# A chain of WKV layers and a graph convolution on one core: r ahead of the sums, inverses and norms ahead of what can wait

## The chip, the cores and the metric

The kernel runs on one core of a Trainium2 chip. The metric is the device time of one execution in microseconds (us); the times shown are medians of several runs. One more execution was taken with the hardware profiler, and all engine times below are from that one. PE is the matrix engine, DVE the vector engine, ACT the scalar engine, POOL is GpSimd, SP issues most DMAs. Each engine works its instructions off in the order of the program and waits for the others by semaphores.

## What is computed

The input x has 16 images of 192 channels and 56 x 56 positions, in float32. Three layers of one kind follow each other, then a graph convolution. Cut to what matters:

```python
xn = group_norm(x, 32)                      # before every layer
k, v, r = xs @ Wk.T, xs @ Wv.T, xs @ Wr.T   # xs: tokens (3136) by channels of xn
x_bi = 0.5 * (wkv(w, u, k, v) + flip(wkv(w, u, flip(k), flip(v))))
h = layernorm(sigmoid(r) * x_bi)
x = x + h @ Wo.T                            # three times, then:
xj = max over rolls by +-2 rows and columns of xn, minus xn, at least 0
x = x + gelu(batchnorm(concat(xn, xj) @ conv_w.T))
```

`wkv` is a running weighted mean over the tokens: numerator p and denominator q are sums of exp(k) v and exp(k) that decay by a constant per channel at every token, and the token itself counts with a bonus.

## The kernel before, in words

Two images make a pair: channels 0 to 127 of each and the two remaining blocks of 64 fill three rows of 128 partitions. The 3136 tokens are cut into seven chunks of 448. A *run* is one layer of one pair. It has a forward pass, chunks 0 to 6 (`A`), that makes exp(k), exp(k) v, the forward scans and their quotient, and a backward pass, chunks 6 to 0 (`B`), that makes r, the backward scans, their quotient, the gate, the layer norm, the output product and the residual. The convolution has one pass of seven chunks (`C`). Eight pairs go in two streams, so that the backward pass of one stream's run stands beside the forward pass or the convolution of the other's.

A written-out list of steps sets the whole order; no scheduler moves anything. Each step calls one of these functions (line numbers of the profile), and the order of the calls in it is the order on every engine:

- `both_a` (L1323), a backward chunk beside a forward chunk: 85 steps, chunks 4 to 0 of a backward pass. `both_a_first` (L1379) is the same for the first pair of chunks of a layer, chunk 5: 17 steps.
- `both_c` (L1426), a backward chunk beside a chunk of the convolution: 42 steps, six a layer, chunks 5 to 0.
- `forward_a`, `forward_c`, `backward_alone`: chunks that have no partner. `conv_part` (L1503) puts halves of delayed convolution products into forward steps.

The pieces that the change moves:

- `b_gate` (L986): PE's product r of a backward chunk, seven matmuls; `b_exp` (L989): ACT's exponentials of it (L996); `b_sigmoid` (L1001): the rest of the sigmoid on ACT (L1003, L978).
- `b_q`, `b_p`, `a_q`, `a_p`: three scans each on DVE (L875). `b_den`, `b_num`, `a_den`, `a_num`: the bonus on DVE (L890). `a_keys`, `a_values`: PE's products k and v; `a_exp` (L920), `a_ekv` (L940) read them.
- `ln` (L974) and `exp_minus` (L977): the inverse as exp(-log) on ACT (L975, L978).
- `b_mix` (L1028): nine products and sums on POOL (L1031 to L1033). `a_y` (L980): one on POOL (L982).
- `b_squares` (L1037): ACT squares (L1040). `b_sums` (L1042): eight matmuls into one bank `st` (L1047, L1049). `b_rs1`: the square of the means on ACT (L1055); `b_rs2`: one matmul that takes it from the mean squares (L1059); `b_rs3`: logarithm and exponential on ACT (L1063, L1065); `b_spread`: three matmuls that spread the result over the partitions (L1071, tile `rsb`); `b_scale`: DVE multiplies (L1076); `b_out`: the output product `ops` on PE; `b_x` (L1085): DVE adds the residual (L1089), SP stores the chunk (L1094).
- `gap` (L822) does one of four parts of the next run's norm: `norm_sums` (DVE, then PE's small product `psg`), `norm_var` (DVE, ACT), `norm_fold` (small operations, then ACT folds the factor into the weights of k and v, L770), `norm_fold_r` (POOL folds it into those of r, L772).
- `c_product`: half of the convolution's product on PE (tile `cv`), with xn or with the maxima; `c_rows`, `c_columns`: the maxima on DVE (L1114 to L1129); `c_gelu`: ACT (L1150), with a load of another function table before and after; `c_add` (L1157): POOL adds x (L1159); `store` (L1172): four DMAs on SP.
- `count` takes statistics of a later pair's input on ACT (L734, L735), up to two thirds of a chunk in a paired step.

PE's results go to seven PSUM banks, handed out in the order of the program; chunks in SBUF take one of 33 slots.

The core of a paired step before, since the prediction follows its order:

```python
        b_gate(*nback[1:]); b_exp(*nback[1:])     # r of the next chunk back
        count(z); b_q(*b)
        b_rs2(*l); b_rs3(*l)                      # l: the chunk of the step before
        b_sigmoid(*b)
        a_values(*a)
        b_spread(*l)
        ...
        b_squares(*b, (1,))
        b_sums(*b)
        ...
        b_rs1(*b)
        invert(den())
```

## Time and profile before

| | |
|---|---|
| median of 3 runs | 5217.34 us (5207.3 to 5221.48) |
| profiled execution | 5220.16 us, span 5218.2 us |
| mean granted clock of PE | 0.935 |
| ACT, POOL busy | 71%, 55% of the span |
| DMA | 482.47 MB, 92 GB/s, queue of SP 28.5% of 16 engines |

The steps can be found in the trace by their instructions. From the first DVE instruction of a step to that of the next they take:

| kind of step | number | mean us | DVE busy in it |
|---|---|---|---|
| both_a | 85 | 25.3 | 24.4 |
| both_a_first | 17 | 30.4 | 27.3 |
| both_c | 42 | 25.3 | 22.3 |
| forward steps (A and C) | 80 | 13.9 | 12.7 |
| backward_alone | 24 | 11.2 | 10.6 |

How to read it: a timeline line holds the start in us, the duration in us, the engine, the line of the kernel, the operation with output, inputs and shapes, and how many instructions were merged; the bracket at its end is the idle time of that engine just before, and what ended it. PEclk is the share of full speed at which PE was clocked in a stretch; 1.00 is full, 0.50 half.

### The profile page before, as it was taken

Reading aid. Unit: us, or ns where it says so; the run is one execution under the profiler, and the core shown is the slowest. Engines: PE = TensorE matmul, PEld = TensorE weight load, DVE = VectorE, ACT = ScalarE, POOL = GpSimd, SP = SyncE. Lnnn points to the kernel's source line nnn. Section 1 sums busy time; section 2 is a strip of 40 time slices with the busy share of each in tenths; the row PEclk is TensorE's granted clock in tenths of the full one; section 3 lists DMA queues with packets and bytes.
Section 4 is the critical chain, followed back from the end, with each engine's and each line's share of the span. In section 5 each row is a group of like instructions: output and inputs, shape, how many; then the busy total and the mean of one; then the engine's idle time right before and its main releaser. Section 6 shows DMA issues by size and latency. Waiting matters only on the chain. (4 is left out here: it accounts for less than half of the span.)

```text
span 5218.2 us, 51856 instructions
## 1 busy us (share of the span) xinstructions
PE 4733.3 (91%) x15542; PEld 1498.8 (29%) x15542; DVE 4750.5 (91%) x6271; ACT 3684.6 (71%) x7163; POOL 2889.2 (55%) x2251
## 2 busy tenths in 40 slices
PE   7899998989899999998989999999898999999897
PEld 3222222223232222222323222222232322222222
DVE  6999999998989999999898999999889899999995
ACT  6777787776566777787656678777756667777772
POOL 1665665554545656565454556556545455666562
PEclk8999999999899999999989999999998999999998
DMA  5222222233232222223233223222333322222233
GB/s 154 69 82 87 90 86 89 85 110 97 90 116 72 87 90 93 82 90 122 93 93 101 84 75 100 88 85 87 128 93 101 93 74 77 72 84 77 80 104 120
DMA packets 314274, 482.47 MB, mean 92 GB/s; under 512 B 66432, under 2 KB 306688, under 8 KB 313984
## 3 DMA queue, kind: packets, MB, share of 16 engines
q1 hardware_dynamic: 312832, 477.59, 28.5%
q8 instruction: 126, 2.06, 0.2%
q10 hardware_dynamic: 1152, 1.48, 0.1%
q14 instruction: 164, 1.34, 0.1%
HBM read 324.83 MB, written 154.14 MB: 92 GB/s over the span
## 5 line engine op out<-in xcount | busy, mean ns | idle before, releaser
L875 DVE TENSOR_TENSOR_SCAN q<-fdecays,ek 128x449 f32<-128x449 f32 (+1 forms) x1008 | 1023.4, 1068 | 28.0 <-ACT ek L920 25.4
L875 DVE TENSOR_TENSOR_SCAN p<-fdecays,ekv 128x449 f32<-128x449 f32 (+1 forms) x1008 | 1020.3, 1065 | 0.6
L982 POOL TENSOR_TENSOR p<-p,q 128x1344 f32<-128x1344 f32 x168 | 512.0, 3047 | 830.3 <-ACT q L978 546.9
L1031 POOL TENSOR_TENSOR ekv<-ekv,ek 128x448 f32<-128x448 f32 x504 | 602.7, 1196 | 456.1 <-ACT ek L978 385.3
L1033 POOL TENSOR_TENSOR p<-p,sg 128x448 f32<-128x448 f32 x504 | 638.0, 1266 | 57.2 <-ACT ek L884 12.7
L1032 POOL TENSOR_TENSOR p<-p,ekv 128x448 f32<-128x448 f32 x504 | 606.1, 1203 | 39.5
L1040 ACT ACTIVATE ek<-p 128x448 f32<-128x448 f32 x504 | 286.4, 572 | 309.4 <-POOL p L1033 308.9
L886 POOL COPY ekv<-p 128x3 f32<-128x3 f32 x282 | 233.1, 827 | 488.0 <-DVE p L875 457.2
L1076 DVE TENSOR_TENSOR p<-p,rsb 128x448 f32<-128x448 f32 x504 | 282.4, 613 | 194.5 <-PE rsb L1071 194.4
L920 ACT ACTIVATE ek<-k,k 128x448 f32<-128x448 f32 x504 | 297.2, 632 | 225.3 <-PE k L601 179.2
L735 ACT ACTIVATE fjunk<-x 128x448 f32<-128x448 f32 x672 | 387.7, 577 | 40.1 <-DVE x L1089 13.4
L1071 PE MATMUL rsb<-rs,fpicks 32*128 32x448 f32 (+1 forms) x1008 | 359.2, 629 | 42.4 <-ACT rs L1065 42.4
L1159 POOL TENSOR_TENSOR ml<-ml,x 128x1344 f32<-128x1344 f32 x56 | 178.9, 3194 | 391.8 <-ACT ml L1150 391.8
L890 DVE SCALAR_TENSOR_TENSOR ek<-ek,fcc,q 128x896 f32<-128x896 f32 x336 | 379.1, 1167 | 0.0
L890 DVE SCALAR_TENSOR_TENSOR q<-ek,fcc,q 128x896 f32<-128x896 f32 x336 | 359.2, 1109 | 6.3 <-ACT cvb L954 4.6
L1089 DVE SCALAR_TENSOR_TENSOR x<-ops,fwob,x 128x448 f32<-128x448 f32 x504 | 314.2, 670 | 46.7 <-PE ops L601 26.6
L734 ACT ACTIVATE fjunk<-x 128x448 f32<-128x448 f32 x600 | 342.5, 571 | 11.4
L996 ACT ACTIVATE sg<-r,r 128x448 f32<-128x448 f32 x504 | 313.0, 627 | 33.5 <-PE r L607 20.7
L890 DVE SCALAR_TENSOR_TENSOR ekv<-ekv,fcc,p 128x896 f32<-128x896 f32 x336 | 330.1, 1022 | 0.0
L940 DVE SCALAR_TENSOR_TENSOR ekv<-v,v,ek 128x448 f32<-128x448 f32 x504 | 312.5, 672 | 16.6 <-PE v L601 8.0
L975 ACT ACTIVATE q<-q 128x1344 f32<-128x1344 f32 x168 | 221.5, 1318 | 125.5 <-DVE q L890 101.3
L890 DVE SCALAR_TENSOR_TENSOR p<-ekv,fcc,p 128x896 f32<-128x896 f32 x336 | 295.3, 919 | 6.5 <-POOL ekv L886 1.7
(235 smaller groups left out, 11546.4 us busy)
## 6 DMA issues: line engine op xcount, KB each, us to landing
x<-xd SPq DMA_DIRECT2D x240, 672.0 KB, 5.3
xd<-x SPq DMA_DIRECT2D x168, 672.0 KB, 3.9
x<-in_x_dram SPq DMA_DIRECT2D x320, 224.0 KB, 4.3
x<-in_x_dram SPq DMA_DIRECT2D x320, 112.0 KB, 4.2
out_dram<-ml SPq DMA_DIRECT2D x112, 224.0 KB, 2.3
m<-xd SPq DMA_DIRECT2D x112, 168.0 KB, 5.1
wkv<-in_wfold_dram SPq DMA_DIRECT2D x24, 640.0 KB, 5.6
out_dram<-ml SPq DMA_DIRECT2D x112, 112.0 KB, 2.3
```

Source lines behind the costliest of these rows:

```text
L734: S.activation(junk, xt[:, j, :], AF.Identity, accum_out=stats[:, 0, j, c : c + 1])
L735: S.activation(junk, xt[:, j, :], AF.Square, accum_out=stats[:, 1, j, c : c + 1])
L875: V.tensor_tensor_scan(out, dec[:, column(j)].to_broadcast([P, L if first else L + 1]), e, 0.0, ALU.mult, ALU.add)
L890: by_channel(lambda js, i: V.scalar_tensor_tensor(dst.t[:, js, :], e.t[:, js, :], cc[:, i : i + 1], state.t[:, js, :], ALU.mult, ALU.add))
L940: V.scalar_tensor_tensor(e.t[:, j, :], ps[j][:, 0:L], b[:, j, :], run.ek[c].t[:, j, :], ALU.add, ALU.mult)
L982: G.tensor_mul(run.h[c].t, run.h[c].t, den.t)
L996: S.activation(sg.t[:, j, :], ps[j][:, 0:L], AF.Exp, bias=b[:, j, :], scale=-1.0, accum_out=run.chk[:, at : at + 1])
L1031: G.tensor_mul(y.t[:, j, :], y.t[:, j, :], den.t[:, j, :])
L1032: G.tensor_add(h.t[:, j, :], h.t[:, j, :], y.t[:, j, :])
L1033: G.tensor_mul(h.t[:, j, :], h.t[:, j, :], sg.t[:, j, :])
L1071: PE.matmul(ps[j][:, :L], pick[rows, j, :], rs[rows, :], start=True, stop=True)
L1089: V.scalar_tensor_tensor(xj, ps[j][:, 0:L], wob[:, column(j)], xj, ALU.add, ALU.add, accum_out=run.new[:, 0, j, c : c + 1] if c == 0 else ...
```

## The change

In `both_a`: r of the chunk after the next (`far`) is computed just ahead of `b_sums`, where it belongs to the same run; `b_gate` skips a chunk that is done. Since only chunks 4, 3 and 2 have such a `far`, chunk 4's step computes two r and those of chunks 1 and 0 none. `a_values` moves ahead of `b_rs2` and `b_rs3`, `count` behind them. The sigmoid moves between the two parts of the inverse, and the forward inverse goes ahead of `b_rs1`.

In `both_a_first` the forward scan and value product go ahead of the denominators, the forward denominator and its inverse ahead of the scaling, the scaling and output product ahead of the next k.

In `both_c` the three gaps (parts of the norm) stand earlier, `b_rs1` and `b_rs2` stand between the logarithm and the exponential of the inverse, and `c_add` behind `b_mix`. In the last step beside a convolution, where a forward pass follows, both halves of its product go to `conv_part`, as those of chunk 6 did before. `fresh` keeps `gap` from folding weights whose load was only just issued.

In `backward_alone` the fold stands right behind the inverse. `c_add` calls `store` before it adds its own result to the list, so that no older result is left there.

```diff
     def gap(eng=V):
-        if norms:
+        if norms and norms[0][0] is norm_fold and norms[0][1] in waiting + fresh:
+            fresh.clear()
+        elif norms:
             part, run = norms.pop(0)
...
     def b_gate(run, c):
-        product(run, "r", run.w[2], run.xb[c], c == NL - 1)
+        if once(run, "r", c):
+            product(run, "r", run.w[2], run.xb[c], c == NL - 1)
...
             require_all(run.chk, slice(3 * NL + 9, NCHK))
+        store()
         stores.append((run, c, g))
...
-    def both_a(b, a, nback, nfront, z, loads):
+    def both_a(b, a, nback, nfront, z, loads, far):
...
-        count(z)
-        b_q(*b)
+        a_values(*a)
         if l:
             b_rs2(*l)
             b_rs3(*l)
-        b_sigmoid(*b)
-        a_values(*a)
+        count(z)
+        b_q(*b)
         if l:
             b_spread(*l)
         b_p(*b)
         b_den(*b)
-        for js in (AC, slice(1, 2)):
-            ln(b[0].ek[b[1]], js)
-            exp_minus(b[0].ek[b[1]], js)
+        ln(b[0].ek[b[1]], AC)
+        exp_minus(b[0].ek[b[1]], AC)
+        b_sigmoid(*b)
+        ln(b[0].ek[b[1]], slice(1, 2))
+        exp_minus(b[0].ek[b[1]], slice(1, 2))
...
         b_squares(*b, (1,))
+        if far:
+            b_gate(*far[1:])
         b_sums(*b)
         a_p(*a)
         gap()
         a_den(*a)
+        invert(den())
         b_rs1(*b)
         late[b] = 0.5
-        invert(den())
         gap()
...
     (both_a_first)
         b_p(*b)
+        a_q(*a)
+        a_save(*a)
+        a_ekv(*a)
+        b_squares(*l, (1,))
         b_den(*b)
         invert(b[0].ek[b[1]])
...
-        a_ekv(*a)
-        b_squares(*l, (1,))
         if nback is not None:
             b_gate(*nback[1:])
         b_sums(*l)
         b_rs1(*l)
+        b_rs2(*l)
+        b_rs3(*l)
         if nback is not None:
             b_exp(*nback[1:])
-        a_q(*a)
-        b_rs2(*l)
-        b_rs3(*l)
+        a_p(*a)
+        a_den(*a)
+        invert(den())
+        spread_and_scale(l)
         keys(nfront)
-        a_p(*a)
-        spread_and_scale(l)
         b_squares(*b, (0,))
-        a_save(*a)
         exp_keys(nfront)
         b_squares(*b, (2, 1))
         b_sums(*b)
-        a_den(*a)
+        a_num(*a)
         b_rs1(*b)
         late[b] = 0.5
-        invert(den())
-        a_num(*a)
         add(l)
...
     (both_c)
             b_out(*l1)
+        gap()
...
         b_den(*b)
-        invert(b[0].ek[b[1]])
+        ln(b[0].ek[b[1]])
+        gap()
         if l0:
             b_rs1(*l0)
             b_rs2(*l0)
+        exp_minus(b[0].ek[b[1]])
+        if l0:
             b_rs3(*l0)
-        gap()
-        if half:
-            u = half.pop()
-            c_gelu(*u, False)
-            c_add(*u)
+        ended = half.pop() if half else None
+        if ended:
+            c_gelu(*ended, False)
...
-        if not first:
+        ahead = l0 and nback is None and nfront is not None and nfront[0] == "A"
+        if not first and not ahead:
             c_product(*a, 0)
         c_rows(*a)
-        gap()
         c_columns(*a)
         gap()
         b_num(*b)
         b_sigmoid(*b)
         b_mix(*b)
+        if ended:
+            c_add(*ended)
...
+        elif ahead:
+            a_q(*nfront[1:])
+            a_save(*nfront[1:])
+            a_values(*nfront[1:])
+            b_scale(*l0)
+            b_out(*l0)
+            late[l0] = 2
+            convs.extend(((a, 0), (a, 1)))
         else:
...
     (backward_alone)
         invert(b[0].ek[b[1]])
+        gap(G)
         b_sigmoid(*b)
         b_p(*b)
-        gap(G)
         b_num(*b)
...
+            far = steps[i + 2][0] if nback is not None and i + 2 < len(steps) else None
+            if far is not None and far[1] is not nback[1]:
+                far = None
```

More of the change, by code (lines that the diff above doesn't have):

```diff
@@ L804, in begin_later @@
         norms.extend((part, run) for part in (norm_sums, norm_var, norm_fold, norm_fold_r))
-    convs, waiting = [], []
+    convs, waiting, fresh = [], [], []
     def load_weights(run):
@@ L1445, in both_c @@
         sum_up()
+        if l1:
+            add(l1)
         if l0:
@@ L1448, in both_c @@
             b_sums(*l0)
-        if l1:
-            add(l1)
         b_den(*b)
-        invert(b[0].ek[b[1]])
+        ln(b[0].ek[b[1]])
+        gap()
         if l0:
@@ L1487, in both_c @@
             half.append(a)
-        else:
-            ahead = nfront is not None and nfront[0] == "A"
-            if ahead:
-                a_q(*nfront[1:])
-                a_save(*nfront[1:])
+        elif ahead:
[6 more added lines that the diff above has]
+            convs.extend(((a, 0), (a, 1)))
+        else:
             c_product(*a, 1)
             c_end(*a, False)
-            if ahead:
-                a_values(*nfront[1:])
             if l0:
@@ L1510, in conv_part @@
                 while waiting:
-                    load_weights(waiting.pop(0))
+                    fresh.append(waiting.pop(0))
+                    load_weights(fresh[-1])
                 return u
@@ L1723, in fast_path @@
             if f and not b and nkeys is None and nfront is not None and i + 2 < len(steps):
-                far = steps[i + 2]
-                if far[0] is None and far[1] is not None and far[1][0] == "A" and far[1][1] is f[1]:
-                    nkeys = far[1]
+                then = steps[i + 2]
+                if then[0] is None and then[1] is not None and then[1][0] == "A" and then[1][1] is f[1]:
+                    nkeys = then[1]
             if f and nback is None and nfront is not None:
@@ L1733, in fast_path @@
                     load_ahead(u)
+            far = steps[i + 2][0] if nback is not None and i + 2 < len(steps) else None
+            if far is not None and far[1] is not nback[1]:
+                far = None
             if b and f and f[0] == "A":
                 if of_stage(0) is None:
-                    both_a(b[1:], f[1:], nback, nfront, z, ahead)
+                    both_a(b[1:], f[1:], nback, nfront, z, ahead, far)
                 else:
```

## The prediction

> **What bounds the kernel now.** I read the page's first part, then the waits, then the timelines of single steps and the stretches cut at them. The page alone shows two engines near their end:

> ```profile
> PE 4733.3 (91%) x15542; PEld 1498.8 (29%) x15542; DVE 4750.5 (91%) x6271; ACT 3684.6 (71%) x7163; POOL 2889.2 (55%) x2251
> ```

> The reader is to see that neither is full. Who sets the end differs by kind of step, so I took stretches: a paired step without input statistics, one with them, and two short ones for the clock (columns: us, then busy time of PE, PEld, DVE, ACT, POOL, then PEclk).

> ```profile
> 1706.30:1729.90 23.60, 23.31 (x82) 7.16 (x84) 23.60 (x31) 19.29 (x38) 15.30 (x12) 1.00 0.27 89
> 1890.60:1917.70 27.10, 25.01 (x82) 7.64 (x80) 25.00 (x30) 21.58 (x45) 15.66 (x12) 0.94 0.22 76
> 1915.60:1919.00 3.40, 3.40 (x10) 1.08 (x11) 3.32 (x5) 1.59 (x3) 0.43 (x1) 0.56 0.00 0
> 1533.70:1540.50 6.80, 6.80 (x12) 2.11 (x14) 6.73 (x11) 3.83 (x12) 0.00 (x0) 0.50 0.48 150
> ```

> The plain step (27 of 85 last 23.6 us) has DVE full for all 23.60 us and PE for 23.31: PE has no room either. The step with statistics (36 of 85 last about 27) has 2 us idle on both, and PE at half clock for some 3.4 us. PE's timeline of that step says why:

> ```profile
> 1888.44 1.53 PE L1049 MATMUL st<-p,fsums 128*32 128x448 f32 x4 [2.08 <-POOL p L1033]
> 1890.69 1.69 PE L598 MATMUL r<-x,wr 128*128 128x448 f32 x2
> ```

> The sums `st` wait 2.08 us for POOL's last product; r stands behind them, r's sigmoid behind r, and POOL's next products behind that on ACT: one ring of 27 us. The gap also costs clock: L598 takes 1.69 here, 1.02 at full clock. The other gaps that the change aims at, in the first step, beside the conv, and in the conv step that folds a norm:

> ```profile
> 1830.34 1.68 DVE L1076 TENSOR_TENSOR p<-p,rsb 128x448 f32<-128x448 f32 x3 [3.36 <-PE rsb L1071]
> ...
> 2466.25 0.96 PE L1059 MATMUL st<-rs,fpicks 64*64 64x448 f32 x2 [1.78 <-ACT rs L1055]
> ...
> 2493.25 0.16 DVE L749 TENSOR_SCALAR nm<-psg 128x3 f32<-128x3 f32 x1 [4.64 <-PE psg L607]
> ```

> And the line that decides my forecast, from a forward step in which PE runs L1059 (`b_rs2`) and L1071 (`b_spread`) back to back:

> ```profile
> 1531.25 0.96 PE L1059 MATMUL st<-rs,fpicks 64*64 64x448 f32 x2
> 1533.54 3.55 PE L1071 MATMUL rsb<-rs,fpicks 32*128 32x448 f32 x6 [1.32 <-ACT rs L1065]
> 1537.01 1.86 PE L598 MATMUL v<-x,wkv 128*128 128x448 f32 x2
> ```

> ACT's logarithm and exponential of `b_rs3` (0.63 + 0.57) leave PE 1.32 us idle, and PE then runs at half clock (0.50 over 6.8 us above): L1071 takes 3.55 instead of 1.97. I followed this order in all forward steps that have it: each time the halved clock came within about 3 us of L1071's start, for 3.4 or 6.8 us.

> [...]L1128 takes 4.44 us at 2496.33, beside POOL's L1159, and 1.56 alone.

> **Prices.** From the plain step's PE timeline: r, v, k, ops 4.5 us each; L1059 0.9; L1071 1.9; the eight sums 1.65 when nothing is late; `b_rs3` makes PE wait 1.32.[...]

> **The change, part by part.**

> *Paired steps.* Removed: the wait of r behind the sums (r of two chunks on goes before them, in the three steps of a layer that have one). Its chunk's load is issued at the same place and lands after 5.3 us; k ends some 10 us later and hides it (uncovered: up to 5.3 a step). Added: `a_values` now goes ahead of `b_rs2`, so PE's order becomes v, L1059, L1071, with nothing between the last two. Before, v stood there and hid `b_rs3`. PE's round is then 1.9 + 4.5 (ops) + 4.5 (k) + 4.5 (r) + 1.65 + 4.5 (v) + 0.9 = 22.5, plus 1.32 = 23.8, plus lost clock. [...]0 to 3.4 us; I take 1.9. Round: 25.7. The logarithms moved ahead of the sigmoid start POOL 2.6 us sooner, which PE cannot use.
> Behind L1071 queue ops, k, r, the sums and all their readers.
> From scale to scale (L1076) the plain layers have 23.7, 23.6, 23.5 us for these three steps, so +2.0, +2.1, +2.2 = +6.3. The layers with statistics have 26.9, 27.1, 27.2: -1.2, -1.4, -1.5 = -4.1. In the last two steps PE has no r, needs 21.2, and DVE's 23.6 hide it: 0.

> *First step.* DVE: the scan and value product of the new layer go ahead of the old layer's denominators (L890), out of POOL's way, and `a_den` fills 1.7 of the 3.36 us gap. PE: L1071 goes ahead of k. Chain at 1806.5: the DVE scans and L940 to 1817.6, L890 (3.1, beside POOL) to 1820.5, ACT's inverse 2.65 and L1055 0.5 to 1823.7, L1059, `b_rs3`, L1071 at 1826.0 (was 1829.3). Then PE owes 1.9 + 0.7 (scale) + 4.5 + 4.5 (k) + 1.65: the sums end at 1839.3, against 1837.4. Two PE waits of over 1 us with L1059 and L1071 between: the clock halves, I take two windows, 3.4. The next step's v, L1059, gap, L1071 adds 0.9 more than before. Sum +2.0 + 3.4 + 0.9 = +6.3 at the second scale.

> There are 17 such layers, 8 plain and 9 with statistics: 8 x (6.3 + 6.3) + 9 x (6.3 - 4.1) = 101 + 20 = **+121**.

> *Conv steps.* L1055 goes between the two halves of the inverse: PE's 1.78 gap loses 1.25. But `c_add` (3.05 on POOL) moves behind the mix and meets DVE's row maxima[...]: 0 to 2.1 us (L1114 takes 0.85 alone, 2.9 on average beside L1159); DVE has some 3 us idle there, so I give 0.25 back. Chunks 3 and 2: -1.0 each; chunk 4: 0, DVE has only 1.5 us idle there. Chunk 1: the norm's sum goes ahead of the conv product, the 4.64 gap and PE's psg behind it go: -5.3. The two late products: PE is full from there through the next four forward steps (steps of 13.5 us of PE work in 12.8), so 9 us are moved, not saved: 0, with -9 as the other bound. L1055 there: -1.2. The fold right after the inverse in the lone backward step passes POOL's save and the sigmoid: k or the conv's first product 2.7 or 1.3 earlier; before a conv -2.5, before a paired layer already in the chain above. On SP the output's four DMAs keep their place at the head of the next step but now wait there for the later add, some 3 us, and the loads of the step queue behind them; those are read a step later: 0. Sum -2.0 - 5.3 - 1.2 - 2.5 = -11.0 a layer, six layers, and -5 in the last, which folds nothing: **-71**.

> **Sum.** Profiled run 5220.2 (span 5218.2, 2.0 around it) + 121 - 71 = 5270. The median of the runs shown is 2.8 lower: 5267.

> **Rivals.**
> *The clock is not lost in paired steps*[...]. For: v and ops on both sides are full-array work, unlike the forward steps, where ops waits once more. Against: six conv-side forward steps have v at once behind L1071 and still lose 6.8 us. Then the first step costs 2.9, plain rounds 23.8 (+0.6 in three), those with statistics ACT and POOL's 25.2 (-5.6): 8 x 3.5 - 9 x 2.7 = +4; total -67, 5150. Faster.
> *The late products pay*: DVE's gaps of 3.7 and 5.5 us behind k and v of the new layer close, and the later steps swallow the products: -9 x 6 on top, 5213. The same.
> *The clock locks* at two windows a round[...]. Plain +17, statistics +7, conv gains halved: 139 + 63 - 35 = +167, 5384. Mine decides against the first rival from 2.6 us lost in a layer's steps on; this is its far end.
> *The change isn't carried out*: excluded, the built order shows v, L1059, L1071.

> **Chances.** Clock lost, as summed: 0.5. Locked: 0.11. Not lost: 0.24. Products pay: 0.15, of which a quarter falls on the fast side of no change. 0.3%, 15 us, is about what can be told from no change. Slower 0.61, same 0.11, faster 0.28. Range: 5150 takes in the first rival's sum, 5335 half of the locked case.

> **What would show it.** Right: gaps of 1.3 us at L1071 in paired steps and PEclk under 0.95 there, no gap at L1049; plain steps of 25 to 26, statistics steps of about 26; DVE idle at L1076 in the second step of a layer; chunk 1 of the conv at 26 instead of 31. Wrong: PEclk 1.00 in plain paired steps, or steps of 23.6 there; the sums still last; conv steps that gain more than 11 us a layer.

## The result and the profile after

The changed kernel takes 5433.52 us (median of 4 runs, 5430.15 to 5435.04), the one before 5212.32 (4 runs, 5199.56 to 5221.48): a ratio of 1.0425, 95% interval 1.0401 to 1.045. It is some 220 us slower; the forecast had 50, and its range ended at 5335.

The page of the changed kernel: span 5432.9 us, mean clock of PE 0.904 (0.935 before).

```profile
PE 4881.7 (90%) x15542; PEld 1539.5 (28%) x15542; DVE 4784.3 (88%) x6271; ACT 3658.5 (67%) x7163; POOL 2867.5 (53%) x2251
...
PEclk8889889899898888899989888889999988899898
```

PE is busy 148 us longer with the same number of matmuls, 15542, at a lower mean clock. DVE was busy 91% of the span and is now busy 88%: that is new waiting. Cutting the trace at the same steps as before shows where both sit (the forecast's terms beside what the steps measured, summed over all layers):

| part | forecast, us | measured, us |
|---|---|---|
| three plain paired steps (chunks 3 to 1), 8 layers | +50 | +54 |
| the same with statistics, 9 layers | -37 | -21 |
| first and second paired step, 8 plain layers | +50 | +67 |
| first and second paired step, 9 layers with statistics | +57 | +116 |
| last paired step and the forward step behind it, 17 layers | 0 | -17 |
| conv steps of six layers, up to the last forward step | -66 | -75 |
| the last forward step of these six | 0 | +88 |
| conv steps of the last layer | -5 | +1 |
| lone steps ahead of the paired layers | 0 | +1 |
| sum | +49 | +214 |

Most rows are near their forecast. Two carry the miss: the first and second step where statistics are taken, and one forward step next to the convolution.

**Paired steps.** Two stretches of the changed kernel, a plain step and one with statistics (us, busy time of PE, PEld, DVE, ACT, POOL, then PEclk):

```profile
1798.10:1825.20 27.10, 25.78 (x91) 7.83 (x90) 23.85 (x31) 18.90 (x38) 15.29 (x12) 0.87 0.23 77
1973.10:2000.20 27.10, 25.78 (x82) 7.99 (x80) 24.61 (x31) 21.33 (x46) 15.29 (x12) 0.87 0.22 76
```

The plain step was 23.60 us at clock 1.00 and DVE full. Now DVE has over 3 us to spare, and PE is busy 25.78 us at 0.87. PE's lines say which wait, here of the step with statistics:

```profile
1976.08 1.02 PE L598 MATMUL v<-x,wkv 128*128 128x448 f32 x2
1980.58 0.96 PE L1063 MATMUL st<-rs,fpicks 64*64 64x448 f32 x2
1982.87 2.85 PE L1075 MATMUL rsb<-rs,fpicks 32*128 32x448 f32 x6 [1.32 <-ACT rs L1069]
1985.65 1.86 PE L598 MATMUL ops<-p,fwo 128*128 128x448 f32 x2
```

This is the order forecast (v, the small product, 1.32 us idle, the spread) with the halved clock behind it: L1075 takes 2.85 where 1.97 is full speed, L598 1.86 where 1.02 is. The old gap at the sums is gone: none of their lines in this step has a bracket.

**First and second step** of a layer with statistics, lines of ACT, PE and DVE in the changed kernel:

```profile
1894.86 3.72 PE L1075 MATMUL rsb<-rs,fpicks 32*128 32x448 f32 x6 [1.32 <-ACT rs L1069]
...
1902.68 0.63 ACT L1000 ACTIVATE sg<-r,r 128x448 f32<-128x448 f32 x1 [7.87 <-POOL p L1036]
...
1904.07 1.86 PE L599 MATMUL ops<-p,fwo 128*128 128x448 f32 x2 [3.70 <-ACT sg L1000]
...
1904.14 1.75 DVE L893 SCALAR_TENSOR_TENSOR p<-ekv,fcc,p 128x896 f32<-128x896 f32 x2 [4.83 <-POOL ekv L889]
...
1930.16 1.15 DVE L1080 TENSOR_TENSOR p<-p,rsb 128x448 f32<-128x448 f32 x2 [10.18 <-PE rsb L1075]
```

Read from the top: the halved clock (3.72 for 1.97) is the forecast's. Then comes a wait that it did not have. ACT stands 7.87 us before r's exponential until POOL has done a product of the mix; until then r's PSUM bank stays full, and `ops` waits 3.70 us for that bank. DVE's old wait of 3.36 us at the spread is now one of 4.83 us at L893, for POOL; that one stands in all 17 layers (3.9 to 5.6 us), so it is not what sets the nine apart. In the step behind, DVE waits 10.18 us for the next spread.

Why ACT waits for POOL: `sg` is written into an SBUF chunk from the list of free ones. By the order of the calls, before the change it got one that the lone step ahead or v's product had left. Now the forward scan and the store of its last value take two chunks ahead of it, and in the nine layers with statistics, where fewer are free, what `sg` gets is the chunk that POOL's mix of the same step gives back (ACT waits 7.9 to 9.1 us). In the eight plain layers it gets the one that v's product left, and ACT does not wait.

**Conv steps.** The two gaps shown of before at PE's L1059 and DVE's L749, in the changed kernel's step of chunk 1:

```profile
2585.41 0.15 DVE L749 TENSOR_SCALAR nm<-psg 128x3 f32<-128x3 f32 x1
...
2589.78 0.96 PE L1063 MATMUL st<-rs,fpicks 64*64 64x448 f32 x2 [0.92 <-ACT rs L1059]
```

The 4.64 us are gone, the 1.78 us are 0.92, and chunk 1's step went from 31.1 to 24.7 us. But in the last forward step of the layer (11.1 us before, 26.4 here) the timeline has

```profile
2713.26 0.33 SPq L813 DMA_DIRECT2D wkv<-in_wcfold_dram  x1
...
2714.99 0.55 SPq L547 DMA_DIRECT2D x<-in_x_dram  x1
...
2719.45 1.83 PE L598 MATMUL k<-x,wkv 128*128 128x448 f32 x2 [6.23 <-DMA x<-in_x_dram]
...
2725.30 3.06 DVE L878 TENSOR_TENSOR_SCAN q<-fdecays,ek 128x449 f32<-128x449 f32 x3 [8.37 <-ACT ek L923]
```

and the waits of SP's queue there say (us in total, times, longest):

```profile
SPq L813 <- PE cv L607: 48.4, 1, 48.4
```

The load of the next run's weights waited 48.4 us on SP for the last convolution product to free its buffer (20.4 us before), and the load of the new layer's last chunk stood behind it: k waits for a DMA, and DVE for k.

One more row hides two waits: chunk 3 beside the convolution takes 28.3 us instead of 24.5 (forecast: -1.0), with

```profile
2535.57 3.67 POOL L1163 TENSOR_TENSOR ml<-ml,x 128x1344 f32<-128x1344 f32 x1
...
2536.25 3.36 DVE L1119 TENSOR_TENSOR m<-m,x 128x336 f32<-128x336 f32 x1
...
2543.49 0.59 DVE L1129 TENSOR_TENSOR ml<-x 128x416 f32<-128x416 f32 x1 [3.46 <-DMA out_dram<-ml]
```

L1119 took 0.50 before (as L1115, with no addition on POOL beside it). The 3.46 us are a matter of chunks again: by the order of the calls, `ml` gets the chunk whose output this step has just sent, and that DMA now starts later, behind the moved addition.

### The profile page after: what moved, and what is told of

It is laid out like the page before. It is cut to its first block, busy times and chain, and to the rows that moved or that the text cites. A ratio compares the mean times of both kernels' runs of the same rounds, so it can differ in the third digit from the quotient of the medians.

```text
span 5432.9 us, 52055 instructions
## 1 busy us (share of the span) xinstructions
PE 4881.7 (90%) x15542; PEld 1539.5 (28%) x15542; DVE 4784.3 (88%) x6271; ACT 3658.5 (67%) x7163; POOL 2867.5 (53%) x2251
## 5 line engine op out<-in xcount | busy, mean ns | idle before, releaser
L1037 POOL TENSOR_TENSOR p<-p,sg 128x448 f32<-128x448 f32 x504 | 621.5, 1233 | 100.9 <-ACT sg L981 50.3
L1036 POOL TENSOR_TENSOR p<-p,ekv 128x448 f32<-128x448 f32 x504 | 589.4, 1169 | 39.5
L1075 PE MATMUL rsb<-rs,fpicks 32*128 32x448 f32 (+1 forms) x1008 | 433.1, 722 | 177.7 <-ACT rs L1069 177.7
L1000 ACT ACTIVATE sg<-r,r 128x448 f32<-128x448 f32 x504 | 311.9, 627 | 123.5 <-POOL p L1037 54.4
L893 DVE SCALAR_TENSOR_TENSOR p<-ekv,fcc,p 128x896 f32<-128x896 f32 x336 | 309.2, 961 | 85.9 <-POOL ekv L889 82.8
L893 DVE SCALAR_TENSOR_TENSOR q<-ek,fcc,q 128x896 f32<-128x896 f32 x336 | 370.6, 1143 | 6.3 <-ACT cvb L957 4.6
L734 ACT ACTIVATE fjunk<-x 128x448 f32<-128x448 f32 x600 | 343.1, 572 | 12.6
L943 DVE SCALAR_TENSOR_TENSOR ekv<-v,v,ek 128x448 f32<-128x448 f32 x504 | 313.5, 675 | 23.8 <-PE v L601 14.5
L893 DVE SCALAR_TENSOR_TENSOR ek<-ek,fcc,q 128x896 f32<-128x896 f32 x336 | 333.3, 1033 | 0.0
L1067 ACT ACTIVATE rs<-st,feps 64x448 f32<-64x448 f32 x168 | 105.6, 628 | 338.2 <-PE st L1063 337.2
L598 PE MATMUL ops<-p,fwo 128*128 128x448 f32 x336 | 262.4, 877 | 35.4 <-DVE p L1080 34.6
L893 DVE SCALAR_TENSOR_TENSOR ekv<-ekv,fcc,p 128x896 f32<-128x896 f32 x336 | 292.1, 911 | 0.0
```

The source lines that it names most:

```text
L598: PE.matmul(ps[0][:, :n], w(0, 0), r(slice(0, P), 0), start=start, stop=False)
L734: S.activation(junk, xt[:, j, :], AF.Identity, accum_out=stats[:, 0, j, c : c + 1])
L893: by_channel(lambda js, i: V.scalar_tensor_tensor(dst.t[:, js, :], e.t[:, js, :], cc[:, i : i + 1], state.t[:, js, :], ALU.mult, ALU.add))
L943: V.scalar_tensor_tensor(e.t[:, j, :], ps[j][:, 0:L], b[:, j, :], run.ek[c].t[:, j, :], ALU.add, ALU.mult)
L1036: G.tensor_add(h.t[:, j, :], h.t[:, j, :], y.t[:, j, :])
L1037: G.tensor_mul(h.t[:, j, :], h.t[:, j, :], sg.t[:, j, :])
```

## The experiments

Ratios are to the kernel before on the same chip; the changed kernel stands at 1.0425. 0.01 is 52 us.

| run | median, us | ratio | interval |
|---|---|---|---|
| weights_load_last | 5393.65 | 1.0351 | 1.0332 to 1.037 |
| sg_own_slot | 5387.98 | 1.0335 | 1.0316 to 1.0353 |
| both_waits_gone | 5343.09 | 1.0247 | 1.0229 to 1.0266 |
| v_behind_rs3 | 5286.34 | 1.0139 | 1.0122 to 1.0156 |
| gap_filled | 5343.01 | 1.0281 | 1.0264 to 1.0298 |
| old_first_step | 5279.09 | 1.0157 | 1.014 to 1.0174 |
| r_ahead_alone | 5260.43 | 1.0119 | 1.0102 to 1.0136 |
| v_first_load | 5055.25 | 0.9729 | 0.9713 to 0.9745 |
| r_and_inverse | 5131.83 | 0.9864 | 0.9847 to 0.988 |
| r_inverse_sigmoid | 5085.04 | 0.9778 | 0.9761 to 0.9794 |
| v_first_no_late | 5061.9 | 0.9731 | 0.9714 to 0.9747 |
| v_load_slot | 5164.05 | 0.9926 | 0.991 to 0.9943 |
| v_first_add_back | 5032.19 | 0.9669 | 0.9656 to 0.9683 |
| add_back | 5406.55 | 1.0395 | 1.0379 to 1.041 |

### The two waits that the forecast lacked

**weights_load_last**, the load behind the last late product:

```diff
-                while waiting:
+                while waiting and not convs:
```

> The changed kernel, with the weights' load of the following run issued only when no delayed convolution product is left (after the fourth of them instead of the second). Theory A (the load's DMA waits on SP until the last convolution product gives its buffer free, 48 us by the trace, and the load of the new layer's last chunk stands behind it): the last forward step of a layer beside a convolution falls from 25-26 us to 11-14, six times, 5433 - 6 x 13 = about 5355. Rival B (the two products that were delayed simply have to be worked off there, 9 us of PE a layer): the step stays over 20 us and the time within 10 us of 5433.

Half of it. 39 us went, by the ratio. The six last forward steps fell from 24.7-26.7 to 17.0-17.7 us, not to 11-14. The wait is gone, as PE's lines show, k right behind the product:

```profile
2704.59 1.02 PE L598 MATMUL cv<-m,wkv 128*128 128x448 f32 x2
2709.10 1.02 PE L598 MATMUL k<-x,wkv 128*128 128x448 f32 x2
```

What stays, some 6 us a layer over before, is late work of PE and the norm's folding, which now falls into this step. So A holds for the wait, and B for the rest.

**sg_own_slot**, in the first step only:

```diff
-    def b_exp(run, c):
+    def b_exp(run, c, own=None):
...
-        sg = run.sg[c] = Slot("sg")
+        sg = run.sg[c] = Slot("sg", own)
...
-            b_exp(*nback[1:])
+            b_exp(*nback[1:], V)
```

> The changed kernel, with r's exponentials in the first paired step of a layer written into a chunk of SBUF that DVE gave free, instead of one that POOL gives free at the end of its mix. Theory A (ACT waits 7.9 us at L1000 for that chunk in the nine layers with statistics, the bank of r stays full, ops waits 3.7 to 4.9 us at L599 for the bank): first and second step lose 5 to 6 us together, 9 x 5.5 = 50, about 5383. Rival B (the first step is late by the order of PE and its halved clock alone, the wait is hidden): within 10 us of 5433.

As A has it: 47 us. In the same first step, ACT and PE:

```profile
1888.20 0.64 ACT L1000 ACTIVATE sg<-r,r 128x448 f32<-128x448 f32 x1
...
1893.53 1.64 PE L599 MATMUL ops<-p,fwo 128*128 128x448 f32 x2
```

No wait stands on either. First and second step of the nine layers now cost 55 us over before, or 6.2 each, where the forecast had 6.3. (In the eight plain layers, which never had this wait, they cost 8.2.)

**both_waits_gone**, both edits.

> The changed kernel with both of the edits before it. Theory A: the two are independent, 5433 - 78 - 50 = about 5305, within 40 us of the forecast 5267, and what is left over 5220 is the clock and the gap at L1075 in the paired steps less what the conv steps gain. Rival B: what one of them frees is lost in the other's place, over 5360.

The two add: 0.0178 together, 0.0074 and 0.009 alone. At 5343 the rest is not yet the forecast: the load's edit gives back half, and the three steps of all layers cost 58 us over before in this run (33 in the changed kernel), though nothing in them was edited.

### The clock and the place of v

**v_behind_rs3**, one line moved in the paired step:

```diff
-        a_values(*a)
         if l:
             b_rs2(*l)
             b_rs3(*l)
+        a_values(*a)
         count(z)
```

> The changed kernel, with v in the paired steps put back between the two small products (L1063, then v, then L1075), one line moved, all else as changed. Theory A (the gap of 1.3 us at L1075 and the halved clock behind it make the plain steps last up to 27 us): plain steps fall from 25.6 on average to 23.6-23.8, the statistics steps from 26.3 to about 25.5, the second step of each layer by 1.3 to 3; 8 x 6.5 + 9 x 2.5 + 17 x 2 = 109, about 5325. Rival B (v ahead of the small products isn't what costs; the three steps are held by the second step's delay): plain steps stay at 25 to 27 us, over 5400.

More than A: 149 us. The three steps last 70.7 us on average, with statistics or without. Plain, then with statistics:

```profile
1753.90:1777.50 23.60, 20.49 (x82) 5.99 (x74) 23.60 (x31) 19.27 (x38) 15.36 (x12) 1.00 0.26 86
1920.40:1944.00 23.60, 22.62 (x84) 7.08 (x80) 23.60 (x31) 21.51 (x46) 15.36 (x12) 1.00 0.26 88
```

DVE is full in both and the clock is 1.00. The step with statistics was 27.1 us before the change: the new paired step, r ahead of the sums with the inverse and the sigmoid moved, gains 10 us in three steps, and v's place takes 8 of them away.

**gap_filled** tells the clock from the gap. A product whose result is overwritten unread goes into the gap:

```diff
+    def fill(run, c):
+        ps = run.ps["rsb"] = banks("rsb")
+        PE.matmul(ps[0][:, :L], params[run.l][5](0, 0), run.h[c].t[:, 0, :], start=True, stop=True)
...
             b_rs2(*l)
+            fill(*l)
             b_rs3(*l)
...
-            b_spread(*l)
+            b_spread(*l, True)
```

> The changed kernel; in the paired steps one full-array product (two matmuls, about 0.9 us, its result is overwritten unread) stands on PE between L1063 and L1075, where PE is idle 1.32 us. It adds work and shortens no wait. Theory A (the idle stretch between the small products halves the clock, and the halved clock is the loss): the clock stays near full in the three steps after the second, plain ones go from 77 us for three to 71-72, those with statistics from 79 to 71-76, 8 x 5.5 + 9 x 5 = 89, about 5345 (5320 to 5385). Rival B (PE loses the 1.32 us and what waits behind it, whatever the clock): nothing is gained, 5425 to 5445.

A: 75 us faster than the changed kernel with one product more in every paired step that has the small products. The order on PE, and then a plain step and one with statistics:

```profile
1778.65 0.96 PE L1063 MATMUL st<-rs,fpicks 64*64 64x448 f32 x2
1779.54 1.02 PE L1073 MATMUL rsb<-p,fwo 128*128 128x448 f32 x2
1780.93 1.97 PE L1080 MATMUL rsb<-rs,fpicks 32*128 32x448 f32 x6 [0.37 <-ACT rs L1069]
```

```profile
1773.20:1797.00 23.80, 23.22 (x84) 6.87 (x76) 23.80 (x31) 18.90 (x38) 15.27 (x12) 1.00 0.24 78
1942.10:1967.40 25.30, 24.93 (x99) 7.76 (x92) 25.22 (x31) 21.52 (x46) 15.52 (x12) 1.00 0.24 83
```

The spread starts no sooner after L1063 (2.28 us, as before the fill), yet runs in 1.97 us, and PEclk is 1.00 in both stretches. Over all layers the three steps' mean clock goes from 0.91 to 0.99 (plain) and 0.97 (with statistics). B, that nothing is gained while PE still waits as long for ACT, is out. But the clock is not all of it: over all layers these steps get 86 us shorter here and 128 in v_behind_rs3, so some 40 stay with the gap, the added product and the clock that is still lost. For most of the clock, filling 0.9 us of the 1.32 us gap was enough.

### The first step

**old_first_step**, `both_a_first` as before the change, whole.

> The changed kernel with the first paired step of a layer in its order of before. Theory A (that step's new order delays the sums and with them the second step: 6 us a layer by PE's order and clock, 6 more in the nine layers with statistics by the wait for a chunk of SBUF): first and second step fall from 63 to 57-58 in plain layers and from 71 to 58 in the others, 8 x 5.5 + 9 x 12.5 = 157, about 5276. Rival B (the second step is late by its own order, v ahead of the small products): only the wait for the chunk goes, as in the run with its own chunk, 5380 to 5390.

A: 140 us by the ratio. First and second step fell by 6.9 us in plain layers and by 12.6 in the others. **v_load_slot** keeps the new first step and mends the rest (the edits of weights_load_last, sg_own_slot and v_behind_rs3).

> The changed kernel with v between the small products, the weights' load behind the last delayed product, and a chunk that DVE gave free for r's exponentials; the first step keeps its new order. Theory A (the new order of the first step costs some 6 us a layer by PE's order and halved clock, apart from the wait for a chunk): 5055 + 17 x 6 = about 5157. Rival B (the wait for the chunk was all that it cost): within 20 us of 5055.

A: 5164, 103 us (0.0197) over the same with the old first step, v_first_load below: 6 us a layer, which the forecast had as 17 x 6.3 = 107. That PE's order and clock make them is read from the trace: from the first step's spread to the end of the second, PE waits for nothing over 0.32 us in 16 of the 17 layers (0.62 in the other), and its clock in the first step is 0.78 to 0.94, against 1.00 in v_first_load. DVE's wait at L893 is still there (3.9 to 5.5 us).

### What r ahead of the sums is worth

**r_ahead_alone**, on the kernel before:

```diff
-        product(run, "r", run.w[2], run.xb[c], c == NL - 1)
+        if once(run, "r", c):
+            product(run, "r", run.w[2], run.xb[c], c == NL - 1)
...
+        if far:
+            b_gate(*far[1:])
         b_sums(*b)
```

> The kernel before with one part of the change: in the paired steps r of two chunks on goes ahead of the sums; v stays between the two small products, everything else as before. Theory A (r behind the late sums is what holds the steps with statistics at 27 us): three steps of those layers fall from 81.2 to 70.8-72, the last paired step of all layers grows by 1.5 as DVE's work moves there, -9 x 10 + 17 x 1.5 = -65, about 5150. Rival B (the steps with statistics are held by ACT and POOL anyway, 25.2 us): -9 x 5 + 25 = -20, about 5195.

Both wrong: slower than before, the plain steps 26.6 us on average instead of 23.6. A plain step's lines:

```profile
1751.87 0.54 ACT L1056 ACTIVATE rs<-st 64x448 f32<-64x448 f32 x1 [4.84 <-PE st L1050]
...
1755.12 3.05 POOL L982 TENSOR_TENSOR p<-p,q 128x1344 f32<-128x1344 f32 x1 [7.71 <-ACT q L978]
...
1755.46 4.26 DVE L890 SCALAR_TENSOR_TENSOR ek<-ek,fcc,q 128x896 f32<-128x896 f32 x2
```

The sums now come after r, 4.5 us later. ACT waits 4.84 us for them at the square of the means, the forward inverse is queued behind that, and POOL's product L982 behind the inverse. It lands on DVE's L890, which takes 4.26 us; in the same step before the two were apart:

```profile
1731.43 3.05 POOL L982 TENSOR_TENSOR p<-p,q 128x1344 f32<-128x1344 f32 x1 [3.68 <-ACT q L978]
...
1735.80 1.71 DVE L890 SCALAR_TENSOR_TENSOR ek<-ek,fcc,q 128x896 f32<-128x896 f32 x2
```

Beside L982 the pair takes 2.55 us more, on the engine that bounds the step: DVE is busy for all 27.00 us of it. In the 24 plain steps L890's pair takes 3.8 us on average instead of 1.7. **r_and_inverse** adds the inverse's move, two lines:

```diff
+        invert(den())
         b_rs1(*b)
         late[b] = 0.5
-        invert(den())
```

> The kernel before with r ahead of the sums and, as the change has it, the forward inverse (L975, L978, 2.65 us on ACT) ahead of the square of the means; nothing else. Theory A (r ahead alone was slower since with r gone from the start of the step nothing on PE covers the inverse that ACT works off between L1056 and the logarithm of the small product: 1.57 us idle at L1072, halved clock): the idle goes, three steps fall from 80 to 71-73 in all layers, 5260 x 0.9975 - 17 x 8 = about 5110. Rival B (POOL's mix starts too late for the sums, whatever stands in ACT's inverse): three steps stay at 78 to 80, over 5220.

133 us faster than r ahead alone (1.0119 to 0.9864), and 1.4% faster than before. Plain: 71 us for three steps; with statistics 74. The amount is A's, its mechanism only in part: in the plain steps of r_ahead_alone PE waited just 0.31 us at the spread, and the collision on DVE was the larger cost there; the 1.57 us are those of the steps with statistics. The edit takes both away at once, so their shares are read from the trace, not tried apart. **r_inverse_sigmoid** has the whole new paired step, v behind the inverse square root:

> The kernel before with the whole paired step of the change, except that v stands between the two small products; first steps, convolution steps and lone steps as before. Theory A: three steps at 70.8 in all layers as in the run with three things mended, 9 x 10.4 + 17 x 1 less 17 x 0.8 for the last step = 97, about 5105; against the run with the inverse alone it shows whether the sigmoid's place counts. Rival B (the gain needs the other changes of the convolution and lone steps too): over 5150.

A: 70.7 us in all layers; the sigmoid's place, together with `count` and the backward scan behind the small products, is worth another 0.0086.

### All mended, and the convolution

**v_first_load**: the edits of v_behind_rs3, old_first_step and weights_load_last.

> The changed kernel with three things put back or mended: v between the small products, the first paired step in its old order, the weights' load behind the last delayed convolution product. Theory A (the three costs are separate and the rest of the change pays): 5433 - 147 - 40 - 17 x 7.3 = about 5120, and at or under the run with r ahead alone less 20. Rival B (the rest of the change, in the convolution's steps, gives nothing once the waits move): at 5150 or over.

Better than A: 0.9729, 2.7% faster than before. The three alone sum to 0.0628, together they bring 0.0696: the second step falls to 25.4 us only when both v's place and the first step are mended. Against r_inverse_sigmoid it has 0.0049 from the other steps.

**v_first_no_late** on top of it, the products put back:

```diff
-        if not first and not ahead:
+        if not first:
             c_product(*a, 0)
...
+            c_product(*a, 1)
+            c_end(*a, False)
             a_values(*nfront[1:])
...
-            convs.extend(((a, 0), (a, 1)))
```

> The run with three things mended, and the two products of the last chunk beside a layer put back in their place, so that only the convolution's last chunk is late, as before. Theory A (the late products are moved and not saved, as forecast: 4.9 and 3.5 us gained in the forward steps, 6.5 given back in the last and 1 to 3 in the convolution steps): within 12 us of 5055. Rival B (they pay 9 us of PE a layer): 5095 to 5110. Rival C (they cost even with the load mended): 5025 or less.

A: 0.9731 against 0.9729. The late products are moved and not saved: the last forward step falls from 17.2 to 12.1 us, and the first forward step grows from 13.9 to 21.8. What they cost in the changed kernel was the queue on SP.

**v_first_add_back**, and **add_back** on the changed kernel: the addition ahead of the mix.

```diff
             c_gelu(*ended, False)
+            c_add(*ended)
...
         b_mix(*b)
-        if ended:
-            c_add(*ended)
```

> The run with three things mended, and the convolution's closing addition on POOL (L1163, 3.05 us) put back right behind the GELU, ahead of the mix. Theory A (put behind the mix it costs in the convolution step of chunk 3: DVE's L1119 takes 3.36 us beside it instead of 0.50, and the maxima wait 3.46 us at L1129 for the output's DMA, which comes later): that step falls from 28.3 to about 24, six or seven times 4 = 26, about 5030. Rival B (put back it meets the maxima of another chunk, as it did before at 4.44 us for L1128): within 10 us of 5055. Rival C (the place behind the mix is what closed the gaps beside chunk 1 and 0): 5070 or more.

> The changed kernel with that addition alone put back ahead of the mix, everything else as changed. Theory A: 26 us less than the changed kernel, a ratio of about 1.0375. Rival B: within 10 us of the changed kernel, 1.0405 to 1.0445.

A in both: 0.9729 to 0.9669, and 1.0425 to 1.0395 (the two intervals of the second pair touch). Chunk 3's step falls by 6.6 us to 21.7, and 4 us come back in other steps. v_first_add_back is the fastest of all, 3.3% under the kernel before, DVE at 94%:

```profile
PE 4650.0 (92%) x15542; PEld 1474.5 (29%) x15542; DVE 4706.0 (94%) x6271; ACT 3671.8 (73%) x7163; POOL 2895.6 (58%) x2251
```

## Why the prediction was wrong

*Direction and main mechanism: right.* Slower, since v ahead of the small products uncovers `b_rs3`, and behind the idle 1.32 us PE runs at half clock (L1075 2.85 us for 1.97). Gaps of 1.32 us at the spread, PEclk under 0.95, hardly a gap at the sums (0.3 us a step with statistics on average, 2.1 before), chunk 1 at 25 instead of 31: as the last section of the forecast asked. gap_filled shows that most of it is the clock. In the windows above the clock goes with the array work more than with PE's busy time. The forecast's figures for lost clock (1.9 us a step, 3.4 in the first) were the author's estimates; before, the stretches at half clock behind this gap in the forward steps lasted 3.4 or 6.8 us, of which half is lost.

*Plain three steps: right in the mean,* +6.8 a layer for +6.3, with some luck. In three of the eight layers all three steps take 27 us, the form of the rival in which the clock locks; in two they take 24. In both_waits_gone and old_first_step, which leave these steps as they are, the mean is +9.3 and +9.0.

*Three steps with statistics: two errors that nearly cancel.* The forecast gave r ahead at most 5.6 us a layer, ACT and POOL being said to need 25.2 us a step. v_behind_rs3 shows 23.6 us, with ACT busy for 21.51 and POOL for 15.36, a gain of over 10 (r ahead with neither inverse nor sigmoid moved, in r_ahead_alone, gave 1.3). And v's place costs 8.2 a layer there, not 1.5. Net -2.3 instead of -4.1.

*First step: a missing wait.* In the layers with statistics the sum for PE's chain came out (6.2 in sg_own_slot, 6.3 in both_waits_gone). The step that failed is the list of what the new order moves: two chunks of SBUF are taken ahead of `sg`, and the chunk that it then gets is POOL's. 47 us. In the plain layers the term was too small, 8.3 for 6.3: the chain was drawn up in a layer with statistics (at 1806.5), and before the change the plain ones had 55.3 us for these two steps, not 58.1.

*Conv steps: one queue missed, and the gain too large.* Without their last forward step they gained 12.5 us a layer for 11.0, but this is no confirmation: the late products leave these steps lighter and are worked off in the one left out. Whole, the layers gain 6.3 each once the load is mended (weights_load_last), 5.7 with the products put back, 8.5 with the addition put back as well as the load mended (v_first_add_back). The step that failed is the pair of zeros, for the two late products and for SP: the forecast followed the outputs' DMAs on SP, not the weights' load, which goes out after the second late product of four and waits for the fourth, with the chunk's load behind it. +88 us in the last forward steps, of which the mended order gives back 39 net. v_first_no_late shows the 0 right for the products themselves.

*The closing addition: mis-sized.* It was bounded at 2.1 us and given 0.25. In chunk 3 the two waits that it brings come to 6.3 us, 2.9 by the collision at L1119 and 3.5 by the output's later DMA, which no term had. Put back, 16 us in the changed kernel and 31 in the mended one, by the ratios.

*The rivals.* The locked clock's 5384 is nearest, but it had 202 us in the paired steps and a conv gain of 35: the paired sum was near (+199), some 50 of it from the chunk. Clock not lost is out. Late products pay is out.

*Open:* which of PE's late work and the norm's folding holds the last forward step at 17 us once the load is mended was read from its lines, not tried apart (with the late products put back it takes 12); nor was the last layer's convolution (+1 for -5). With both missing waits gone the kernel still stands 78 us over the forecast's sum. By its steps 45 are in the three paired steps, 15 in the plain first and second steps and 28 in the conv steps, against some 20 gained at the last paired ones; why the clock is lower in the three steps there (0.88 and 0.87, plain and with statistics) than in the changed kernel (0.91 in both) is not known.

## What to carry to other kernels

When a call is moved, list not only its instructions but what it takes from shared stocks (chunks, banks) and what its DMAs wait for: a load that was issued early waited 48.4 us on SP here, with everything behind it. Before moving the work that fills a wait between small matmuls, find what else fills it; here even a filler whose result nobody reads was worth 75 us. Parts of one change can hide each other: here the same change holds a gain of 2 to 3% and a loss of 7.

## What was not expected of the hardware

One useless product a step made the kernel 1.4% faster than the changed one (1.0281 for 1.0425), at an unchanged start of the spread. The clock went with the array work in windows of 3.413 us (of 261 under 35%, 252 were followed by half clock), more than with PE's busy time (of 149 windows 60 to 70% busy, three quarters). And r ahead of the sums, a move on PE alone, stretched DVE's L890 from 1.71 to 4.26 us by way of ACT and POOL.
